# Fetching a channel's shifted columns one channel ahead, in three tiles, in the last stage of a four-layer convolution kernel

## The chip, the cores and the metric

The kernel runs on one core of one Trainium2 chip. The metric is the device time of one execution in microseconds (us). A core has five engines that run side by side, each with its own instruction queue: PE (matrix multiplication; PEld is its loading of weights), DVE (vector work), ACT (scalar functions and scaled copies), POOL (further vector work) and SP, which issues the transfers (DMA). An engine takes its queue in order: an instruction that waits holds everything behind it.

## What is computed

The input `x` has 32 images of 192 channels of 56 x 56 points, float32. Four layers follow, each of the form x + layer(group norm of x):

```python
x = x + _L0_conv_ref(_gn(x), ...)   # agent attention with a depthwise convolution
x = x + _L1_conv_ref(_gn(x), ...)   # scan in both directions (RWKV)
x = x + _L2_conv_ref(_gn(x), L2_conv_offset)
x = x + _L3_conv_ref(_gn(x), ...)   # long convolution, by Fourier transforms
```

Only layers 2 and 3 matter here; the last stage of the kernel computes both. Layer 2 shifts each group of four channels by whole rows and columns (zeros come in from outside) and smooths the result with a 3 x 3 Gaussian:

```python
out = jax.vmap(shift_one, in_axes=(1, 0, 0, 0), out_axes=1)(x, yc, xc, mask)
kern = jnp.exp(-sq / (2.0 * SIGMA ** 2))
kern = kern / kern.sum(axis=(1, 2), keepdims=True)
out_LO = jax.lax.conv_general_dilated(out, kern, ..., feature_group_count=Cn)
```

Layer 3 multiplies the two-dimensional spectrum of each channel by that of a 55 x 55 filter, transforms back, cuts out 56 x 56 and adds a bias times the input. The group norm before it takes mean and variance over six channels, so six channels make one group, and there are 32 groups.

## The kernel before

`all_blocks` (L1797) runs the filter, the attention and the scan first, which are not touched, and then `channel_blocks` (L1507), which begins at about 8360 us. Its 192 channels are worked on one by one. A tile holds one channel of all images: 114 partitions (two half-sets of images, each with 56 rows and one row of zeros) and 16 x 56 numbers in each.

For each channel the stage does this:

- `prepare(c)` (L1590). SP brings the channel into a tile `shifted` with its columns already displaced, by reading the source from another address (L1610). Where the displacement has brought in numbers of the neighbouring row, a second transfer writes zeros over them (L1613). It overwrites part of what the first wrote, so it waits until the first has landed. POOL multiplies the tile by the scale of the norm (L1614). ACT makes the first of three taps along the columns into a tile `smooth` (L1617). For the two other taps ACT makes a tile `more` (L1623) and POOL adds it to `smooth` (L1624); for channels 0, 2 and 4, DVE does both at once (L1620). `matrix` (L1552), once for four channels, builds the matrix that displaces the rows and taps along them.
- `shift` (L1628). SP loads the channel itself into a tile `x` (L1633), PE multiplies `smooth` by that matrix (L1639), DVE adds the product to `x` (L1640) and sums (L1641).
- `centre` (L1657). When all six channels of a group are shifted, DVE subtracts the mean into a tile `padded` (L1659), ACT squares it into `sq` (L1661) and DVE sums the squares (L1662).
- `analyse` (L1670) of the group before. PE transforms `padded` (L1785 in `_rows_to_spectra`, emptied from PSUM by ACT, L1791, and L1681), and DVE multiplies by the filter's spectrum in six instructions (L1688 to L1694).
- `synthesise` (L1697). PE transforms back (L1707, emptied from PSUM by ACT, L1715, and L1726), DVE adds to `x` (L1727), and SP stores the result by two transfers (L1730).

The loop at L1746 runs over groups and, inside, over six steps j. In step j it analyses channel j of the group before, synthesises the channel before that, shifts channels 2j and 2j + 1 of its own group while j < 3 (the shift half), centres two channels when j is 3 or more (the centre half), and prepares the channel four ahead of the step's number. Channels 0 to 3 are prepared ahead of the loop (L1744).

This order in the source is not the order of execution. A scheduler puts the instructions of every engine into a fixed order when the kernel is built: it takes what its own estimates of durations say is ready, earlier lines first. It also puts in the waits. Buffers matter to it: a tile that is made anew waits until the last use of the tile whose place it takes. There are two `shifted` tiles, taken in turn by channel number; five `smooth` tiles; three of the tag `spare`, which `more` and `sq` share; eight `padded` tiles, taken in turn; fifteen `x` tiles; and four PSUM tiles `ps`, which L1639, L1707, L1726, L1650, L1565 and L1785 share.

Of the kernel before, what the change touches and what calls it, by code (L numbers as in the profile page):

```python
# [20 lines left out]
F32 = mybir.dt.float32  # L21
# [7 lines left out]
C = 192  # L29
T = 96  # L30
S = 56
# [14 lines left out]
GROUP = C // 32  # L46
# [120 lines left out]
def _bc(ap, shape):  # L167

    return ap.unsqueeze(len(ap.shape)).to_broadcast(shape)
# [1337 lines left out]
def channel_blocks(ctx: ExitStack, tc: tile.TileContext, shifts, k, flat_x2, x2, rs2, spectra, out):  # L1507
# [10 lines left out]
    NI, NG = NB // 2, NB // 4  # L1518
    cp = ctx.enter_context(tc.tile_pool(name="d_c", bufs=1))
    xp = ctx.enter_context(tc.tile_pool(name="d_x", bufs=15))  # L1520
    wp = ctx.enter_context(tc.tile_pool(name="d_w", bufs=2))
# [3 lines left out]
    PR, NP = 2 * (S + 1), C // 4  # L1525
# [7 lines left out]
    for rows, shape in CHANNEL:  # L1533
        n = int(np.prod(shape))
        t = fixed[:rows, at : at + n]
# [2 lines left out]
    f1, f2, f3, f4, ones, ones_u, lags, diff_y, _ = pieces  # L1538
    eps = cp.tile([PR, 1], F32, name="eps", tag="eps")
    nc.vector.memset(eps, GN_EPS)  # L1540
    padded = [cp.tile([PR, NI, 64], F32, name=f"padded{i}", tag=f"padded{i}") for i in range(8)]
    for t in padded:
        nc.gpsimd.memset(t[:, :, S:64], 0.0)

    shifted = [cp.tile([PR, 2 * S * (NI + 2)], F32, name=f"shifted{i}", tag=f"shifted{i}") for i in range(2)]
    zeros = cp.tile([PR, S], F32, name="zeros", tag="zeros")
    for t in (*shifted, zeros):
        nc.gpsimd.memset(t, 0.0)
# [3 lines left out]
    def matrix(n):  # L1552

        if n not in made:
            engine = nc.vector if n < 2 else nc.gpsimd
            t = [wp.tile([PR, PR], F32, name=f"tap{f}", tag=f"tap{f}", bufs=1) for f in range(3)]
            for f in range(3):
                engine.tensor_scalar(
                    t[f], diff_y, found[:, n, 6 + f : 7 + f], found[:, n, 3 + f : 4 + f], ALU.is_equal, ALU.mult
                )  # L1560
            mat = wp.tile([PR, PR], F32, name="mat", tag="mat", bufs=3)
            engine.tensor_tensor(t[0], t[0], t[1], ALU.add)
            engine.tensor_tensor(mat, t[0], t[2], ALU.add)
            ps = psum()
            nc.tensor.matmul(ps[:PR, :PR], lags, mat, start=True, stop=True)  # L1565
            rows = wp.tile([PR, PR], F32, name="rows", tag="rows", bufs=3)
            nc.vector.tensor_copy(rows, ps[:PR, :PR])
            made.clear()
            made[n] = rows
        return made[n]  # L1570
# [7 lines left out]
    def begin(n):  # L1578
        q = Group()
        q.n, q.x, q.padded = n, [], []  # L1580
        q.scale = scales[n]
        q.g = sp.tile([84, GROUP, 2, 42], F32, name="g", tag="g")
        nc.sync.dma_start(out=q.g, in_=spectra[:, n * GROUP : (n + 1) * GROUP])
        q.sums = sp.tile([PR, 2, GROUP, NI], F32, name="sums", tag="sums")
        return q

    begin_at, scales, smooth, rows_of = {}, {}, {}, {}
    SPAN = PR * NI * S

    def prepare(c):  # L1590

        if c >= C:
            return
        n, j = divmod(c, GROUP)
        if j == 0:
            scales[n] = sp.tile([PR, GROUP, NI], F32, name="scale", tag="scale", bufs=3)
            for s in range(2):
                nc.sync.dma_start(
                    out=scales[n][(S + 1) * s : (S + 1) * (s + 1)],
                    in_=rs2[c : c + GROUP, s].partition_broadcast(S + 1),  # L1600
                )
        i = c // 4
        if c % 4 == 0:
            begin_at[i] = nc.values_load(
                begins[0:1, i : i + 1], engines=(mybir.EngineType.SP,), min_val=LEAD - S, max_val=LEAD + S
            )
        wide = shifted[c % len(shifted)]
        t = wide[:, 2 * S - 1 : 2 * S - 1 + 2 * S * NI].rearrange("p (g w) -> p g w", w=2 * S)[:, :, 0 : S + 2]
        there = flat_x2[bass.ds(begin_at[i] + c * SPAN, SPAN)].rearrange("(p g w) -> p g w", p=PR, w=S)
        nc.sync.dma_start(out=t[:, :, 1 : S + 1], in_=there)  # L1610

        bare = wide[:, bass.ds(LEAD + S - begin_at[i], 2 * S * (NI + 1))].rearrange("p (g w) -> p g w", w=2 * S)
        nc.sync.dma_start(out=bare[:, :, 0:S], in_=zeros.unsqueeze(1).to_broadcast([PR, NI + 1, S]))  # L1613
        nc.gpsimd.tensor_tensor(t, t, _bc(scales[n][:, j], [PR, NI, S + 2]), ALU.mult)  # L1614
        y = wp.tile([PR, NI, S], F32, name="smooth", tag="smooth", bufs=5)
        taps = [found[:, i, f : f + 1] for f in range(3)]
        nc.scalar.activation(y, t[:, :, 0:S], AF.Copy, scale=taps[0])  # L1617
        for f in (1, 2):
            if c < GROUP and c % 2 == 0:
                nc.vector.scalar_tensor_tensor(y, t[:, :, f : f + S], taps[f], y, ALU.mult, ALU.add)  # L1620
                continue
            more = wp.tile([PR, NI, S], F32, name="more", tag="spare", bufs=3)
            nc.scalar.activation(more, t[:, :, f : f + S], AF.Copy, scale=taps[f])  # L1623
            nc.gpsimd.tensor_tensor(y, y, more, ALU.add)  # L1624
        smooth[c] = y
        rows_of[c] = matrix(i)

    def shift(q, j):  # L1628

        c = q.n * GROUP + j  # L1630
        rows = rows_of.pop(c)
        x = xp.tile([PR, NI, S], F32, name="x", tag="x")
        nc.sync.dma_start(out=x, in_=x2[c].rearrange("s h g w -> (s h) g w"))  # L1633
        flat, y = x.rearrange("p g w -> p (g w)"), smooth.pop(c).rearrange("p g w -> p (g w)")
        for g0 in range(0, NI, 8):
            n = min(8, NI - g0)
            px = slice(g0 * S, (g0 + n) * S)
            ps = psum()
            nc.tensor.matmul(ps[:PR, : n * S], rows, y[:, px], start=True, stop=True)  # L1639
            nc.vector.tensor_tensor(flat[:, px], flat[:, px], ps[:PR, : n * S], ALU.add)  # L1640
        nc.vector.tensor_reduce(q.sums[:, 0, j, :], x, AX.X, ALU.add)  # L1641
        q.x.append(x)
        yield
# [21 lines left out]
    def spread(q):  # L1665
        q.rs = sp.tile([84, NI], F32, name="rs", tag="rs")
        nc.scalar.activation(q.rs, means(q, 1, ones_u), AF.Ln, bias=eps[:84])
        nc.scalar.activation(q.rs, q.rs, AF.Exp, scale=-0.5)
# [65 lines left out]
    def centres(q, j):  # L1734

        if j == 0:
            middle(q)
        centre(q, j)
        yield

    before, ending = None, iter(())
    for c in range(4):  # L1744
        prepare(c)
    for n in range(C // GROUP + 1):  # L1746
        q = begin(n) if n < C // GROUP else None
        for j in range(GROUP):
            two = [iter(()), iter(())]
            if q is not None:  # L1750
                two = [shift(q, 2 * j + i) if j < 3 else centres(q, 2 * j - 6 + i) for i in range(2)]
            taking = analyse(before, j) if before is not None else iter(())
            for step in (
                taking, two[0], taking, ending, ending, two[0], taking, ending, ending, two[1], taking,
                ending, two[1], ending,
            ):
                next(step, None)
            prepare(n * GROUP + j + 4)
            for rest in (*two, taking, ending):
                for _ in rest:  # L1760
                    pass
            ending = synthesise(before, j, before.product) if before is not None else iter(())
        if q is not None:
            spread(q)
        before = q
# [161 lines left out]
```

## Time and profile before

| what | us |
|---|---|
| median of three runs | 12290.15 |
| lowest and highest | 12282.31, 12302.48 |
| the profiled execution's own time | 12293.47 |
| its span, first to last instruction | 12291.7 |
| the channel stage in it, 8360 to the end | 3931.7 |
| PE, DVE, ACT, POOL busy in that stage | 3612.9, 3304.2, 2305.2, 1393.9 |
| from one group of six channels to the next, in the steady part | 119.3 |

The span is the sum of all stages, so the share of busy time over the whole of it says little of this one; the rows for the channel stage do. Idle time of an engine is named with what ended it, its releaser. A wait of an engine costs nothing unless another engine then stands still for it. SP's transfers are shown by the time of their issue and the time of landing.

### The profile page before, as it was taken

Reading aid. Unit: us, or ns where it says so; the run is one execution under the profiler, and the core shown is the slowest. Engines: PE = TensorE matmul, PEld = TensorE weight load, DVE = VectorE, ACT = ScalarE, POOL = GpSimd, SP = SyncE. Lnnn points to the kernel's source line nnn. Section 1 sums busy time; section 2 is a strip of 40 time slices with the busy share of each in tenths; the row PEclk is TensorE's granted clock in tenths of the full one; section 3 lists DMA queues with packets and bytes.
Section 4 is the critical chain, followed back from the end, with each engine's and each line's share of the span. In section 5 each row is a group of like instructions: output and inputs, shape, how many; then the busy total and the mean of one; then the engine's idle time right before and its main releaser. Section 6 shows DMA issues by size and latency. Waiting matters only on the chain. (4 is left out here: it accounts for less than half of the span.)

```text
span 12291.7 us, 158148 instructions
## 1 busy us (share of the span) xinstructions
PE 11099.2 (90%) x57358; PEld 6662.0 (54%) x57358; DVE 10776.0 (88%) x14739; ACT 7125.1 (58%) x14684; POOL 3379.2 (27%) x2551
## 2 busy tenths in 40 slices
PE   7999999999999999888888888886999999999999
PEld 3555555655555555333333333333666666666666
DVE  6888888888888887999999999995888888888887
ACT  3555555555555554566666666664565656656565
POOL 0000000000000000655655555553333433333330
PEclk9999999999999999899999999997999999999999
DMA  2111111111111111244344433444333333333331
GB/s 70 40 42 45 51 41 40 40 40 40 40 40 40 42 48 46 75 103 99 95 98 103 101 95 96 103 101 105 86 85 84 88 84 89 83 87 87 83 89 41
DMA packets 1652785, 881.51 MB, mean 72 GB/s; under 512 B 1492833, under 2 KB 1529972, under 8 KB 1642860
## 3 DMA queue, kind: packets, MB, share of 16 engines
q1 hardware_dynamic: 1641756, 845.59, 27.3%
q10 hardware_dynamic: 10240, 25.70, 0.8%
q8 instruction: 458, 7.50, 0.3%
q14 instruction: 331, 2.71, 0.1%
HBM read 482.13 MB, written 240.85 MB: 59 GB/s over the span
## 5 line engine op out<-in xcount | busy, mean ns | idle before, releaser
L617 DVE SCALAR_TENSOR_TENSOR o<-v_a,att_w,o 128x896 f32<-128x896 f32 (+1 forms) x1024 | 1056.6, 1032 | 418.5 <-ACT v_a L591 291.5
L1131 POOL MEMSET f<- 128x1 f32 x96 | 8.8, 98 | 4726.4 <-DMA st_c<-st 4721.4
L1791 ACT COPY y<-ps 64x252 f32<-64x252 f32 (+1 forms) x2376 | 805.3, 339 | 569.7 <-PE ps L1785 539.7
L1624 POOL TENSOR_TENSOR smooth<-smooth,more 114x896 f32<-114x896 f32 x378 | 864.3, 2289 | 909.7 <-ACT more L1623 832.9
L1707 PE MATMUL ps<-fixed,real 84*84 84x112 f32 x6144 | 1097.1, 260 | 0.9 <-ACT y L1791 0.9
L1707 PE MATMUL ps<-fixed,imag 84*84 84x112 f32 x6144 | 1094.1, 260 | 0.0
L1715 ACT ACTIVATE z<-ps,rs 84x112 f32<-84x112 f32 x3072 | 808.3, 356 | 250.2 <-PE ps L1707 247.2
L1707 PEld LDWEIGHTS ps<-fixed,real 84*84 84x84 f32 x6144 | 793.8, 154 | 163.6 <-issue 131.8
L1124 ACT ACTIVATE q<-q 128x784 f32<-128x784 f32 x384 | 328.3, 855 | 807.6 <-DVE q L1119 638.2
L1707 PEld LDWEIGHTS ps<-fixed,imag 84*84 84x84 f32 x6144 | 769.0, 154 | 0.0
L879 PE MATMUL ps<-sq,fixed 128*128 128x392 f32 x512 | 302.0, 753 | 427.3 <-ACT sq L1202 427.3
L634 ACT ACTIVATE pr<-ps,low 98x896 f32<-98x896 f32 (+1 forms) x384 | 352.0, 917 | 560.8 <-DVE low L632 560.1
L1614 POOL TENSOR_TENSOR shifted<-shifted,scale 114x928 f32<-114x928 f32 x192 | 362.8, 1889 | 1106.4 <-DMA shifted<-zeros 1070.0
L1785 PE MATMUL ps<-fixed,padded 114*128 114x168 f32 x3072 | 533.0, 325 | 138.9 <-DVE x L1727 135.5
L617 DVE SCALAR_TENSOR_TENSOR o<-v_c,att_w,o 128x448 f32<-128x448 f32 (+1 forms) x1024 | 638.1, 623 | 5.0
L630 PE MATMUL ps<-xs_a,gk_a 128*98 128x448 f32 (+1 forms) x1536 | 637.0, 495 | 0.0
L1726 PE MATMUL ps<-z,fixed 84*114 84x448 f32 x1536 | 619.2, 544 | 15.4 <-ACT z L1715 14.8
L631 PE MATMUL ps<-xs_c,gk_c 125*98 125x448 f32 (+1 forms) x1536 | 631.6, 492 | 0.0
L722 PE MATMUL ps<-gq_a,xs_a 128*112 128x294 f32 x1792 | 603.4, 418 | 19.3 <-DVE pq L727 19.3
L879 PE MATMUL ps<-x,weights 128*128 128x392 f32 x1536 | 573.2, 516 | 28.6 <-DVE bv L1153 14.3
L723 PE MATMUL ps<-gq_c,xs_c 125*112 125x294 f32 x1792 | 595.1, 413 | 0.0
L1785 PEld LDWEIGHTS ps<-fixed,padded 114*128 114x128 f32 x3072 | 481.3, 200 | 208.7 <-DVE x L1727 158.5
(377 smaller groups left out, 29242.6 us busy)
## 6 DMA issues: line engine op xcount, KB each, us to landing
x<-x SPq DMA_DIRECT2D x576, 392.0 KB
x<-x SPq DMA_DIRECT2D x512, 196.0 KB
shifted<-zeros SPq DMA_DIRECT2D x192, 423.9 KB
shifted<-x SPq DMA_DIRECT2D x192, 399.0 KB
x<-x SPq DMA_DIRECT2D x192, 399.0 KB
out_x<-x SPq DMA_DIRECT2D x384, 196.0 KB
x<-in_x SPq DMA_DIRECT2D x32, 1568.0 KB
x<-x SPq DMA_DIRECT2D x32, 1568.0 KB
```

The source lines that it names most:

```text
L617: nc.vector.scalar_tensor_tensor(dst, tap(i), dww[:, t, i : i + 1], dst, ALU.mult, ALU.add)
L630: mm(ps[P2, h, :n], g[:, cols], xs_a[j][:, px], start=True, stop=False)
L631: mm(ps[P2, h, :n], gk_c[0:KC, 2 * j + h, cols], xs_c[j][0:KC, px], start=False, stop=True)
L722: mm(ps[:SUB, i, :HA], xs_a[j][:, px], g, start=True, stop=False)
L723: mm(ps[:SUB, i, :HA], xs_c[j][0:KC, px], gq_c[0:KC, 2 * j + (q + i) // ns], start=False, stop=True)
L879: mm(out, aa, srcs[t][h], start=True, stop=False)
L1624: nc.gpsimd.tensor_tensor(y, y, more, ALU.add)
L1707: nc.tensor.matmul(ps[:84, i * 2 * S : (i + 1) * 2 * S], part[:, i0 + i].rearrange("p s u -> p (s u)"), f3[:, m, :], start=(m == 0), stop= ...
L1715: nc.scalar.activation(z[:, i0 + i].rearrange("p m w -> p (m w)"), ps[:84, i * 2 * S : (i + 1) * 2 * S], AF.Copy, scale=q.rs[:, i0 + i : i ...
L1726: nc.tensor.matmul(got, f4[:, m, :], z[:, i0 : i0 + n, m, :], start=(m == 0), stop=(m == 1))
L1785: nc.tensor.matmul(ps[:, g * 168 : (g + 1) * 168], flat[:, (g0 + g) * 128 : (g0 + g + 1) * 128], f1, start=True, stop=True)
L1791: nc.scalar.copy(y[64 * m : 64 * m + 64, 2 * g0 + i : 2 * (g0 + n) : 2], got[64 * i : 64 * i + 64, :, :, m, :])
```

## The change

`prepare` is cut in two. `fetch(c)` has the scale's loads, the address, the columns and the zeros. `prepare(c)` has the multiplication, the taps and the matrix. `fetch(0)` stands ahead of the loop; after that each `prepare(c)` has a `fetch(c + 1)` before it. The tiles `shifted` become three; the tiles `padded` become seven and `smooth` four. In each partition a `shifted` tile has 8064 bytes, a `padded` one 4096 and a `smooth` one 3584.

```diff
-    padded = [cp.tile([PR, NI, 64], F32, name=f"padded{i}", tag=f"padded{i}") for i in range(8)]
+    padded = [cp.tile([PR, NI, 64], F32, name=f"padded{i}", tag=f"padded{i}") for i in range(7)]
...
-    shifted = [cp.tile([PR, 2 * S * (NI + 2)], F32, name=f"shifted{i}", tag=f"shifted{i}") for i in range(2)]
+    shifted = [cp.tile([PR, 2 * S * (NI + 2)], F32, name=f"shifted{i}", tag=f"shifted{i}") for i in range(3)]
...
-    def prepare(c):
+    fetched = {}
+
+    def fetch(c):
 
         if c >= C:
             return
...
         nc.sync.dma_start(out=bare[:, :, 0:S], in_=zeros.unsqueeze(1).to_broadcast([PR, NI + 1, S]))
+        fetched[c] = t
+
+    def prepare(c):
+
+        if c >= C:
+            return
+        n, j = divmod(c, GROUP)
+        i, t = c // 4, fetched.pop(c)
         nc.gpsimd.tensor_tensor(t, t, _bc(scales[n][:, j], [PR, NI, S + 2]), ALU.mult)
-        y = wp.tile([PR, NI, S], F32, name="smooth", tag="smooth", bufs=5)
+        y = wp.tile([PR, NI, S], F32, name="smooth", tag="smooth", bufs=4)
...
     before, ending = None, iter(())
+    fetch(0)
     for c in range(4):
+        fetch(c + 1)
         prepare(c)
...
+            fetch(n * GROUP + j + 5)
             prepare(n * GROUP + j + 4)
```

## The prediction

> **What bounds the kernel now.** I read the page first, for the share of the stage and for the chain, then the busy times by stretch, then who waited for whom, and last the timeline of one group of six channels. From the page, engine totals and the lines of the chain:
>
> ```profile
> PE 11099.2 (90%) x57358; PEld 6662.0 (54%) x57358; DVE 10776.0 (88%) x14739; ACT 7125.1 (58%) x14684; POOL 3379.2 (27%) x2551
> PE ps L1707 4%; DMA shifted<-zeros 3%; DMA shifted<-x 3%; PE ps L1726 2%; PE re L1681 2%; PE ps L1785 2%; PE im L1681 2%; PE ps L1639 1%; DVE imag L1694 1%; DVE real L1690 1%; POOL shifted L1614 1%; POOL smooth L1624 1%; DVE padded L1659 1%; ACT y L1791 1%; DVE a L1693 1%
> ```
>
> 6% of 12291.7 us, some 740 us, of the chain are the two transfers that the change moves. That is not what they are worth: the chain follows the last arrival, and a path beside it can be nearly as late. So the busy times of the channel stage (us; PE, PEld, DVE, ACT, POOL busy; clock; DMA share, GB/s), first 28 groups of its steady part, then its start, then a stretch near the end where almost no preparing is left:
>
> ```profile
> 8716.00:12070.00 3354.00, 3154.74 (x18334) 2204.29 (x18333) 2909.68 (x4289) 2031.68 (x5464) 1231.32 (x699) 0.97 0.36 86
> 8373.00:8603.00 230.00, 139.56 (x616) 89.37 (x616) 136.44 (x193) 99.05 (x209) 111.40 (x74) 0.73 0.42 105
> 12075.00:12186.00 111.00, 110.12 (x680) 79.19 (x679) 95.34 (x155) 60.05 (x184) 6.16 (x3) 1.00 0.14 28
> ```
>
> PE is idle for 3354.0 - 3154.7 = 199 us of the steady part, 7.1 us in a group of 119.3 us (spacing of the loads of `g`). More than that no wait can give back. DVE is at 87%. The waits of the same 28 groups (engine, line, releaser: us, times, longest) name what makes up the 199 us, and what ACT stands still for:
>
> ```profile
> PE ps L1785 <- DVE x L1727: 126.4, 53, 4.5
> PE ps L1639 <- ACT z L1715: 29.4, 39, 2.1
> PE ps L1639 <- DVE x L1727: 15.9, 23, 1.2
> PE ps L1639 <- POOL smooth L1624: 9.2, 13, 0.8
> PE ps L1639 <- ACT y L1791: 6.5, 14, 2.2
> PE ps L1726 <- ACT z L1715: 5.8, 7, 2.2
> ACT smooth L1617 <- POOL shifted L1614: 439.5, 118, 7.3
> DVE sums L1662 <- ACT sq L1661: 48.0, 57, 1.2
> ```
>
> ACT stands 439.5 us (15.6 a group) in front of the first tap for a multiplication that is not done; behind it in its queue stand the copies that empty PSUM. PE, though, loses only 29.4 + 6.5 + 5.8 = 42 us to ACT (1.5 a group), and 142 us to DVE. One channel on the chain (start, us, what):
>
> ```profile
> 9287.66 6.29 DMA shifted<-x
> 9293.96 6.60 DMA shifted<-zeros
> 9300.70 1.77 POOL shifted L1614
> ```
>
> and POOL and ACT in the timeline at such a place (start, us, instruction, idle before it and releaser):
>
> ```profile
> 9580.22 2.21 POOL L1614 TENSOR_TENSOR shifted<-shifted,scale 114x928 f32<-114x928 f32 x1 [8.52 <-DMA shifted<-zeros]
> 9582.46 1.06 ACT L1617 ACTIVATE smooth<-shifted,found 114x896 f32<-114x896 f32 x1 [5.23 <-POOL shifted L1614]
> ```
>
> Zeros follow columns and the multiplication the zeros, 14.7 us in all; ACT, idle for 5.23 us, starts as POOL ends. The zeros cannot overlap the columns of the same tile, since they overwrite part of them.
>
> **The skill.** "DMA: Bandwidth & Descriptors", "Why a DMA increments its semaphore by 16 and not by 1": a transfer uses the largest number of engines up to 16 that divides its outer dimension; for 114 rows I work out 6. No view here shows engines one by one; 399 KB in 6.3 us agrees with a slow transfer. "SBUF — State Buffer", "Who interferes with whom": a DVE instruction with two SBUF inputs contends with a GpSimd one that reads SBUF. The trace agrees: L1694 takes 578 ns at least, 2496 at most, and about 2 us where POOL adds run beside it. "Perfetto Trace Analysis", "Identifying the Most-Contended Engine", warns that matmul busy share is no measure of roofline; I use gaps, not the share.
>
> **Step 1, columns and zeros start earlier.** Columns of channel c now wait for the tile of c-3 instead of c-2 (its last `more`, L1623). In the trace the columns of 63, 64, 65, 66 start at 9528.6, 9543.4, 9564.6, 9567.4, each within 0.1 us of the end of the last `more` of c-2. But tiles plus `smooth` tiles are seven before (2 + 5) and after (3 + 4). Where taps wait for `smooth`, the transfer's start is not earlier; the taps are one shift later (bursts of six shift matmuls, L1639, 10.5 us apart). Either way some 10 us lie between data and need, against 14.7 us plus SP's queue. I count the ACT stall as gone to seven tenths, not whole: POOL's order is fixed beforehand, and a multiplication placed too early still holds the adds behind it (L1624), which free `spare`. Worth: 0.7 x 1.5 = 1.1 us of PE a group. Of the 1.7 us a group for which DVE waits for `sq` (48.0/28) I take 0.3 as PE time, for DVE has no other idle there. Bounds: 0, and 1.5 + 1.7.
>
> **Step 2, `smooth` 5 to 4.** The first tap of c waits for the shift matmul of c-4, not c-5. For the fifth channel of a group the tap moves from 9558.7 to after its group's first shift (9574 to 9577). It is needed at 9615, its adds take 2 x 2.3 us after 3 x 1.05 us of ACT: over 25 us in hand, nothing late. Added wait: ACT for PE; behind it stand PSUM copies of matmuls that come after that shift anyway, so I take 0. Bounds: -0.3 (nothing in its place) to +0.5 us of PE for each of six passes, the second if PE is short of PSUM just then (four `ps`, and L1639 <- ACT already waits 2.1 us at the longest).
>
> **Step 3, POOL's adds of that channel move.** 4.6 us of L1624 leave the last tenth of the group, where DVE has no idle and PE 0.4 us, for the first shift, where DVE waits 1.6 us per 10 us. The durations of DVE's instructions above the tenth percentile of their own line and shape add up to 12.9 us a group; that is a third of a us per us of POOL in the centre half, a quarter in the shift half: -1.5 us of DVE there, +1.15 here. In PE time I take -0.3 and +0.3: 0.
>
> **Step 4, `padded` 8 to 7.** Centring channel c now waits for the analysis of c-7, an iteration (20 us) earlier: 0. If that were late, DVE would hold the centre half: up to +1 us a group.
>
> **Step 5, SP's queue.** The same 192 column and 192 zero transfers (0.85 us of issue each), moved one channel up, past x loads (L1633), scales and one pair of stores (L1730). The zeros' wait for landing (6.3 us) holds SP as before. The store may come some us later; x tiles are 15 deep and loads run up to 138 us ahead of their shift (9436.0 for 9574.2), so 0. Cover gone, each late load would cost its wait of 2.5 us (344.9/138).
>
> **Step 6, start and end.** From 8373 to 8603 the chain is columns, zeros, multiplication over and over, a new channel every 11 to 12 us. Three tiles let a third transfer queue up, but two issued back to back land about 4.2 us apart (the multiplications of channels 0 and 1, each waiting for its zeros, start at 8388.6 and 8392.8): 8.4 us a channel, and a load of x, for which I take 2.5 between 0 and 4.2. That is near 11 us, so the queue of transfers is nearly full. Group 0 gains 0; group 1 gains 1 us x 6 = 6. The third memset is 1.78 us on POOL, idle 2.6 us before its first multiplication: 0. After the last channel nothing changes.
>
> **Sum.** Steady: 1.1 + 0.3 = 1.4 us x 31 groups = 43, start 6: 49 us. Own time of the profiled execution 12293.5 (span 12291.7, 1.8 us around it) - 49 = 12244; that execution lies 3.3 us over the median of 12290.15, so 12241 for the median.
>
> **Rivals.** *Hidden anyway:* PE's largest wait, 126.4 us, is for DVE in the centre half, which no transfer touches; PE then waits a little longer there and the gain is under 24 us: 12280 (a fifth of 49 kept). For it: 142 of 199 us are DVE's. Against: the 42 us are PE's own idle, and nothing else fills them.
> *Other side, taps in step with PE:* each first tap now stands in ACT's queue behind a shift matmul, while that matmul needs a PSUM tile that ACT must empty. At 0.5 us for each of six passes, 3.0 us a group, less the 1.4 gained: 1.6 x 31 = 50 less 6 at the start, 44 slower: 12334. It decides from 1.4/6 = 0.23 us a pass. For it: L1639 is already where ACT's lateness hits PE. Against: what stands behind the tap mostly needs later matmuls.
> *More gained:* all 42 us of ACT, half of the `sq` wait, and the start by 20 us as group 1 closes up (its 8473 to 8603 is 130 us against 119): 42 x 31/28 + 27 + 20 = 93, 12197. For it: near the end, with no preparing, PE is at 110.1 of 111 us. Against: there POOL is quiet too.
> *Not what it says:* the order on the engines is fixed beforehand by estimated durations, and the transfers could be put no earlier; that is the first rival's time.
>
> **Chances.** Forecast 0.46 (own range 12200 to 12265), hidden 0.22, slower 0.23, more gained 0.09. A measurement of this kernel tells about 0.2%, 25 us, from no change. Faster 0.46 + 0.09 = 0.55; same 0.22; slower 0.23. The range runs from 12185, within the last case, to 12325, into the slower case, leaving about 0.17 out.
>
> **What would show it.** Right: ACT's wait at the first tap for the multiplication falls from 15.6 us a group below 5, PE's waits for ACT below 0.6, group spacing near 117.9 us. Step 2 wrong: ACT's first tap waits for L1639, and PE's L1639 for ACT above 1.5 us a group. Step 3 wrong: L1694 grows. Step 5 wrong: x loads land after their shift is due. Wrong as a whole: spacing unchanged although the ACT wait is gone.

## The result, and the profile after

| | before | after |
|---|---|---|
| median, us (5 runs each) | 12289.5 | 12355.6 |
| lowest and highest | 12282.3, 12302.5 | 12338.3, 12358.8 |
| ratio, 95% interval | | 1.0051 [1.0036, 1.0065] |
| span of the profiled execution | 12291.7 | 12336.5 |
| from one load of `g` to the next, mean of 29 groups | 119.47 | 121.19 |

The change made the kernel slower by about 0.5%, 63 us by the ratio or 66 by the medians. First the engine totals and the lines of the chain from the page of the changed kernel. Line numbers have moved: the first tap is now L1626, the passes into `more` L1632, the adds L1633, the multiplication L1623, the shift's matmul L1648, PSUM's copies L1803 and L1724.

```profile
PE 11099.2 (90%) x57358; PEld 6656.5 (54%) x57358; DVE 10766.9 (87%) x14739; ACT 7141.9 (58%) x14684; POOL 3323.3 (27%) x2551
...
PE ps L1716 6%; PE ps L1735 2%; PE re L1690 2%; PE im L1690 2%; DMA shifted<-zeros 2%; DMA shifted<-x 2%; ACT y L1803 2%; PE ps L1797 2%; PE ps L1648 2%; DVE padded L1668 1%; DVE imag L1703 1%; POOL smooth L1633 1%; DVE real L1699 1%; DVE sums L1671 1%; DVE a L1702 1%; DVE a L1701 1%
```

The two transfers have gone from 6% of the chain to 4%, as the change meant, and the time went up all the same. PE's busy time over the whole program is the same to 0.1 us, but that hides a difference. In the channel stage the same 20832 matmuls are busy for 3627.7 us instead of 3612.9: 15 of the 50 us by which the stage grew, counted from its load of `found`. The other 35 us are idle time of PE, in which the waits show; the last section comes back to the 15. The channel stage, and then the same steady stretch as before the change, in the columns of the prediction:

```profile
8360.00:12336.50 3976.50, 3627.68 (x20832) 2531.85 (x20832) 3295.19 (x4897) 2321.96 (x6202) 1393.80 (x811) 0.95 0.35 83
...
8716.00:12070.00 3354.00, 3121.58 (x18007) 2178.78 (x18007) 2850.30 (x4213) 2008.09 (x5362) 1205.83 (x687) 0.96 0.36 84
```

In the steady stretch PE is busy 33 us less in the same time. The waits in it (engine, line, releaser: us, times, longest), ACT's first, then PE's:

```profile
ACT more L1632 <- POOL smooth L1633: 313.7, 87, 9.9
...
ACT smooth L1626 <- PE ps L1648: 17.3, 36, 0.7
...
PE ps L1797 <- DVE x L1736: 106.5, 44, 5.0
PE ps L1648 <- ACT y L1803: 38.1, 14, 4.3
PE ps L1648 <- POOL mat L1563: 35.5, 11, 4.8
PE ps L1648 <- ACT z L1724: 25.5, 28, 2.4
PE ps L1648 <- DVE x L1736: 13.6, 31, 1.1
PE ps L1648 <- POOL smooth L1633: 8.2, 3, 7.0
```

The wait of 439.5 us at the first tap for the multiplication is off the list. In its place stands one that the kernel before did not have: ACT waits 313.7 us at `more` for POOL's adds. And PE, which lost 61 us in front of the shift's matmul, now loses 121 there; its idle time in the stretch went from 199 to 232 us, from 7.1 to 8.4 us a group.

The timeline of ACT over the first shifts of a group shows how (start, us, instruction, idle before it and releaser):

```profile
9554.99 2.00 ACT L1632 ACTIVATE more<-shifted,found 114x896 f32<-114x896 f32 x2
...
9557.81 1.07 ACT L1632 ACTIVATE more<-shifted,found 114x896 f32<-114x896 f32 x1
...
9568.90 1.06 ACT L1626 ACTIVATE smooth<-shifted,found 114x896 f32<-114x896 f32 x1
9573.29 1.06 ACT L1632 ACTIVATE more<-shifted,found 114x896 f32<-114x896 f32 x1 [3.33 <-POOL smooth L1633]
...
9589.29 1.05 ACT L1632 ACTIVATE more<-shifted,found 114x896 f32<-114x896 f32 x1 [7.51 <-POOL smooth L1633]
9590.25 4.21 ACT L1803 COPY y<-ps 64x252 f32<-64x252 f32 x12
```

POOL in the same stretch:

```profile
9569.03 1.76 POOL L1623 TENSOR_TENSOR shifted<-shifted,scale 114x928 f32<-114x928 f32 x1 [12.65 <-DMA shifted<-zeros]
9570.75 4.92 POOL L1633 TENSOR_TENSOR smooth<-smooth,more 114x896 f32<-114x896 f32 x2
9585.02 1.76 POOL L1623 TENSOR_TENSOR shifted<-shifted,scale 114x928 f32<-114x928 f32 x1 [9.36 <-DMA shifted<-zeros]
9586.74 4.67 POOL L1633 TENSOR_TENSOR smooth<-smooth,more 114x896 f32<-114x896 f32 x2
```

Read it from the top. At 9554.99 ACT makes both `more` tiles of channel 64, but its first tap has no `smooth` tile yet: that tile is held until the group's first shift, and the tap runs at 9568.90. Nothing can be added to a tap that is not there, so the two `more` tiles are held for about 14 us before the first add can start. At 9557.81 channel 65 takes the third and last tile of the tag `spare`. Its second pass has to wait for an add of channel 64. The adds of 65 in turn stand in POOL's queue behind a multiplication, two channels later, that waits 9.36 us for its transfer. So ACT stands 7.51 us, and behind it the copies that empty PSUM. Four of them end at about 9591.7, and PE starts its third shift:

```profile
9591.82 2.74 PE L1648 MATMUL ps<-smooth,rows 114*114 114x448 f32 x4 [3.08 <-POOL mat L1563]
```

Its releaser is given as a POOL instruction that ends at 9591.80, but that is a coincidence. In the trace the entry of PE's queue just ahead of this matmul waits for a counter (a semaphore) of ACT from 9587.91 to 9591.77, and it is ACT's fourth copy, ending at 9591.72, that raises this counter; POOL's is asked for only after it. It is the same for all 11 waits put down to L1563 and the three put down to L1633, and for the 13 put down to L1624 in the kernel before. So of the 121 us in front of the shift's matmul 107 are waits for copies by ACT (38.1 + 35.5 + 25.5 + 8.2), where it was 45 of 61. None of them is left in e6 below, where POOL still makes the same matrices.

### The profile page after: what moved, and what is told of

Same layout as the page of the kernel before. It is cut to its first block, busy times and chain, and to the rows that moved or that the text cites. A ratio compares the mean times of both kernels' runs of the same rounds, so it can differ in the third digit from the quotient of the medians.

```text
span 12336.5 us, 158145 instructions
## 1 busy us (share of the span) xinstructions
PE 11099.2 (90%) x57358; PEld 6656.5 (54%) x57358; DVE 10766.9 (87%) x14739; ACT 7141.9 (58%) x14684; POOL 3323.3 (27%) x2551
## 3 DMA queue, kind: packets, MB, share of 16 engines
q14 instruction: 331, 2.71, 0.1%
## 5 line engine op out<-in xcount | busy, mean ns | idle before, releaser
L1803 ACT COPY y<-ps 64x252 f32<-64x252 f32 (+1 forms) x2376 | 805.3, 339 | 604.2 <-PE ps L1797 574.5
L1633 POOL TENSOR_TENSOR smooth<-smooth,more 114x896 f32<-114x896 f32 x378 | 879.0, 2325 | 769.6 <-ACT more L1632 650.0
L1724 ACT ACTIVATE z<-ps,rs 84x112 f32<-84x112 f32 x3072 | 811.4, 356 | 353.8 <-PE ps L1716 352.0
L1623 POOL TENSOR_TENSOR shifted<-shifted,scale 114x928 f32<-114x928 f32 x192 | 355.0, 1849 | 1344.9 <-DMA shifted<-zeros 1320.6
L1649 DVE TENSOR_TENSOR x<-x,ps 114x448 f32<-114x448 f32 x384 | 236.7, 619 | 401.9 <-PE ps L1648 366.9
```

The costliest lines, as they stand in the source:

```text
L1724: nc.scalar.activation(z[:, i0 + i].rearrange("p m w -> p (m w)"), ps[:84, i * 2 * S : (i + 1) * 2 * S], AF.Copy, scale=q.rs[:, i0 + i : i ...
L1803: nc.scalar.copy(y[64 * m : 64 * m + 64, 2 * g0 + i : 2 * (g0 + n) : 2], got[64 * i : 64 * i + 64, :, :, m, :])
```

## The experiments

Theory A put the loss on the fourth `smooth` tile, theory B on the third `shifted` tile with the earlier transfers. All ratios are to the kernel before, run on the same chip beside it.

| run | what it is | ratio, 95% interval | median, us | before there |
|---|---|---|---|---|
| changed kernel | the change as it stands above | 1.0051 [1.0036, 1.0065] | 12355.6 | 12289.5 |
| e1 | before, with 4 `smooth` | 1.0073 [1.0059, 1.0086] | 12385.9 | 12294.4 |
| e2 | changed, with 5 `smooth` and 14 `x` | 0.9991 [0.9985, 0.9998] | 12283.0 | 12294.4 |
| e3 | tiles as before, transfers ahead in the source | 0.9998 [0.9989, 1.0006] | 12292.5 | 12294.4 |
| e4 | tiles as changed, transfers not ahead in the source | 1.0032 [1.0019, 1.0046] | 12339.5 | 12294.4 |
| e5 | changed, adds ahead of a later multiplication on POOL | 0.9952 [0.9939, 0.9966] | 12241.1 | 12302.8 |
| e6 | changed, passes into `more` behind the first tap on ACT | 0.9904 [0.9889, 0.9919] | 12181.1 | 12302.8 |
| e7 | changed, with 4 `spare` and 14 `x` | 0.9920 [0.9905, 0.9936] | 12200.6 | 12302.8 |
| e8 | e2 with e6's order | 0.9929 [0.9915, 0.9942] | 12215.5 | 12302.8 |
| e9 | before, with e6's order | 0.9998 [0.9989, 1.0007] | 12294.8 | 12295.2 |
| e10 | e1 with e6's order | 0.9917 [0.9900, 0.9933] | 12191.0 | 12295.2 |
| e11 | changed, with the orders of e5 and e6 | 0.9933 [0.9916, 0.9949] | 12213.2 | 12295.2 |
| e12 | before, with 14 `x` | 0.9996 [0.9987, 1.0004] | 12287.1 | 12295.2 |

### The parts of the change one by one: e1 to e4

e1 is the kernel before with one number changed:

```diff
-        y = wp.tile([PR, NI, S], F32, name="smooth", tag="smooth", bufs=5)
+        y = wp.tile([PR, NI, S], F32, name="smooth", tag="smooth", bufs=4)
```

> The kernel before with four smooth tiles instead of five, nothing else: two shifted tiles, eight padded tiles, no separate fetch. Theory A (the fourth smooth tile makes the loss: taps wait for the shift of four channels earlier, the multiplications stand ahead of the adds on POOL, and ACT waits for the adds): slower than before by 40 to 90 us, and ACT's wait for L1624 at L1623 appears, 200 us or more in the 28 steady groups, against 0 before. Theory B (three tiles and the earlier transfers make the loss, by putting multiplications that wait for a transfer earlier into POOL's queue): within 20 us of before.

It alone is slower by 0.73%, at least as much as the whole change (the two intervals overlap a little). The waits of e1, ACT's and then PE's:

```profile
ACT more L1623 <- POOL shifted L1614: 247.2, 56, 8.8
...
ACT more L1623 <- POOL smooth L1624: 65.0, 30, 2.6
...
PE ps L1639 <- ACT y L1791: 72.4, 14, 5.5
PE ps L1639 <- POOL tap L1558: 70.7, 13, 6.4
```

The size is at the upper end of what theory A said. The wait for the adds is only 65.0 us, not 200; most of ACT's time at `more` is spent on the multiplication, since with two `shifted` tiles it too comes late. Both stand at the passes into `more`, with the copies for PSUM behind them in ACT's queue; of PE's 70.7 us put down to L1558, 66.6 are again waits for ACT's copies. So held `spare` tiles are not the larger wait of e1. What it shares with the changed kernel is the order on ACT: for 89 of the 192 channels, in both traces, ACT makes two or three passes into `more` before the first tap of that channel (its own two, and sometimes one of the next). In the kernel before it makes one, for 30 channels. PE and DVE have the same order in e1 as before. That ACT's order carries the loss of e1 is what e10 below shows; by which of its waits was not taken apart.

e2 is the changed kernel with the fifth tile back, and the room for it taken from the `x` tiles:

```diff
-    xp = ctx.enter_context(tc.tile_pool(name="d_x", bufs=15))
+    xp = ctx.enter_context(tc.tile_pool(name="d_x", bufs=14))
...
-        y = wp.tile([PR, NI, S], F32, name="smooth", tag="smooth", bufs=4)
+        y = wp.tile([PR, NI, S], F32, name="smooth", tag="smooth", bufs=5)
```

> The changed kernel with five smooth tiles again, room for it taken from the x tiles (14 instead of 15). Theory A: the loss is gone, 12230 to 12295 us, and what the earlier transfers are worth alone shows: ACT's wait for the multiplication at the first tap under 150 us in 28 groups. Theory B: slower than before by 40 us or more, as in the changed kernel.

The loss is gone, and what is left of the change is worth 0.09%. Its waits show why no more:

```profile
ACT more L1632 <- POOL shifted L1623: 117.7, 28, 5.7
...
PE ps L1648 <- ACT z L1724: 71.8, 28, 4.6
```

The wait at the first tap has moved to a `more` pass, once a group, and once a group PE loses 2.6 us. Here too passes stand ahead of their tap, for 59 channels.

e3 has the transfers ahead in the source, but two `shifted`, eight `padded` and five `smooth` tiles; e4 has the tiles of the changed kernel, and the transfers back in `prepare`.

```diff
# e3, against the changed kernel
-    padded = [cp.tile([PR, NI, 64], F32, name=f"padded{i}", tag=f"padded{i}") for i in range(7)]
+    padded = [cp.tile([PR, NI, 64], F32, name=f"padded{i}", tag=f"padded{i}") for i in range(8)]
...
-    shifted = [cp.tile([PR, 2 * S * (NI + 2)], F32, name=f"shifted{i}", tag=f"shifted{i}") for i in range(3)]
+    shifted = [cp.tile([PR, 2 * S * (NI + 2)], F32, name=f"shifted{i}", tag=f"shifted{i}") for i in range(2)]
...
-        y = wp.tile([PR, NI, S], F32, name="smooth", tag="smooth", bufs=4)
+        y = wp.tile([PR, NI, S], F32, name="smooth", tag="smooth", bufs=5)
# e4, against the kernel before
-    padded = [cp.tile([PR, NI, 64], F32, name=f"padded{i}", tag=f"padded{i}") for i in range(8)]
+    padded = [cp.tile([PR, NI, 64], F32, name=f"padded{i}", tag=f"padded{i}") for i in range(7)]
...
-    shifted = [cp.tile([PR, 2 * S * (NI + 2)], F32, name=f"shifted{i}", tag=f"shifted{i}") for i in range(2)]
+    shifted = [cp.tile([PR, 2 * S * (NI + 2)], F32, name=f"shifted{i}", tag=f"shifted{i}") for i in range(3)]
...
-        y = wp.tile([PR, NI, S], F32, name="smooth", tag="smooth", bufs=5)
+        y = wp.tile([PR, NI, S], F32, name="smooth", tag="smooth", bufs=4)
```

> The transfers stand a channel ahead in the source, but with two shifted tiles, eight padded and five smooth tiles as before. Theory A: within 20 us of before, since the tile decides when the transfer can start, not the place in the source. Theory B, if the place in the source counts: slower by 20 us or more.

> Three shifted tiles, seven padded and four smooth tiles as in the changed kernel, but the transfers stay with the multiplication in the source. Theory A: like the changed kernel, 12335 to 12370 us, since tiles and smooth are the same. Theory B, if the place in the source counts: at least 30 us faster than the changed kernel.

Where the transfers stand in the source does nothing (e3), and without it the changed kernel's tiles are nearly as slow (e4; its interval and the changed kernel's overlap). The tile decides when a transfer can start. So the change is, for the chip, a third `shifted` tile paid for with a `smooth` tile, and the payment costs more than the tile brings: +0.73% in e1, of which e4, with the third tile, keeps +0.32%. The number of `padded` tiles was not varied alone; e2 has seven and no loss.

### How the fourth tile costs time: e5, e6, e7

Three edits to the changed kernel, each on another link of the loop seen in the timeline. In the traces PE and DVE have the order of the changed kernel in all three, and in e7 POOL too. e5 puts the multiplication of channel c behind the second add of channel c-2 in POOL's queue:

```diff
-        nc.gpsimd.tensor_tensor(t, t, _bc(scales[n][:, j], [PR, NI, S + 2]), ALU.mult)
+        if c - 2 in added:
+            with tc.issue_after(added.pop(c - 2).ins):
+                nc.gpsimd.tensor_tensor(t, t, _bc(scales[n][:, j], [PR, NI, S + 2]), ALU.mult)
...
-            nc.gpsimd.tensor_tensor(y, y, more, ALU.add)
+            added[c] = nc.gpsimd.tensor_tensor(y, y, more, ALU.add)
```

> The changed kernel, with each multiplication (L1623) put into POOL's queue behind the second add (L1633) of the channel two before it; PE and DVE keep their orders. Theory A1 (with four smooth tiles the loss is that adds stand on POOL behind a multiplication that waits for its transfer): at least half of the 61 us is healed, 12325 us or less, and ACT's wait for L1633 falls from 313.7 us in 28 groups below 120. Theory A2 (the loss is that two more tiles are made ahead of the first tap and hold the spare tiles): less than 20 us healed.

e6 puts the passes into `more` behind the first tap of the same channel in ACT's queue:

```diff
-        nc.scalar.activation(y, t[:, :, 0:S], AF.Copy, scale=taps[0])
+        first = nc.scalar.activation(y, t[:, :, 0:S], AF.Copy, scale=taps[0])
...
-            nc.scalar.activation(more, t[:, :, f : f + S], AF.Copy, scale=taps[f])
+            with tc.issue_after(first.ins):
+                nc.scalar.activation(more, t[:, :, f : f + S], AF.Copy, scale=taps[f])
```

> The changed kernel, with the two more passes (L1632) put into ACT's queue behind the first tap (L1626) of the same channel; PE and DVE keep their orders. Theory A2: at least half of the 61 us is healed, 12325 us or less, and ACT's wait for L1633 falls below 120 us in 28 groups. Theory A1: less than 20 us healed.

e7 has a fourth `spare` tile and 14 `x` tiles:

```diff
-            more = wp.tile([PR, NI, S], F32, name="more", tag="spare", bufs=3)
+            more = wp.tile([PR, NI, S], F32, name="more", tag="spare", bufs=4)
...
-        sq = wp.tile([PR, NI, S], F32, name="sq", tag="spare", bufs=3)
+        sq = wp.tile([PR, NI, S], F32, name="sq", tag="spare", bufs=4)
```

> The changed kernel with four spare tiles instead of three, room from the x tiles (14 instead of 15); POOL, PE and DVE keep their orders. Both A1 and A2 pass through the spare tiles, so both expect ACT's wait for L1633 to fall below 200 us in 28 groups and 15 to 45 us healed. If that wait is not what PE loses by (theory A3: the late tap itself, or the matrix for the shift standing on POOL), the wait falls and the time stays within 10 us of the changed kernel.

All three heal more than the whole loss: from +0.51% to -0.48%, -0.96% and -0.80%. The two readings between which e5 and e6 were to decide, the adds behind a waiting multiplication (A1) and the `more` tiles made ahead of the tap (A2), are not rivals, then, but links of one loop, and any of them opens it. e7 was expected to gain 15 to 45 us and gained about 160. ACT's wait for the adds, 313.7 us in the changed kernel, is 124.9 in e5 and 123.0 in e7 (a near miss of the bound of 120 in e5), and in e6 it is 1.0, once. ACT in e6, over the shifts of a group:

```profile
9541.87 1.06 ACT L1626 ACTIVATE smooth<-shifted,found 114x896 f32<-114x896 f32 x1 [0.43 <-PE ps L1649]
9542.84 1.98 ACT L1633 ACTIVATE more<-shifted,found 114x896 f32<-114x896 f32 x2
9547.64 4.22 ACT L1804 COPY y<-ps 64x252 f32<-64x252 f32 x12 [2.83 <-PE ps L1798]
9551.89 1.06 ACT L1626 ACTIVATE smooth<-shifted,found 114x896 f32<-114x896 f32 x1
```

and what is left of its waits, ACT's first tap and then PE:

```profile
ACT smooth L1626 <- PE ps L1649: 24.8, 57, 0.4
...
PE ps L1798 <- DVE x L1737: 134.7, 53, 5.1
PE ps L1649 <- DVE x L1737: 10.6, 26, 0.9
PE re L1691 <- ACT y L1804: 3.5, 23, 0.2
```

The tap waits at most 0.4 us for its shift, its passes come after it, and PE loses 3.5 us to ACT in the whole stretch, where it lost 44 in the kernel before (the 42 of the prediction, and 2.6 in front of L1681; 53 with the 9.2 put down to L1624). POOL still waits 1181.9 us for transfers in e6, against 1196.4 in the changed kernel: no cost of that wait is to be seen once ACT hardly waits for an add behind it.

### What the order and the tiles are worth apart: e8 to e12

The edits are those shown already, in other company: e8 is e2 with e6's edit of the order; e9 is the kernel before with it; e10 is e1 with it; e11 is the changed kernel with the edits of e5 and e6; e12 is the kernel before with 14 `x` tiles, the control for e2, e7 and e8.

> The changed kernel with five smooth tiles, 14 x tiles, and the two more passes behind the first tap in ACT's queue; only ACT's order differs from e2. In e2 ACT waits 117.7 us in 28 groups at L1632 for the multiplication, and PE's L1648 waits 71.8 us for ACT's L1724. If the first is what makes the second, this version is 15 to 60 us faster than e2 and beats both kernels, 12225 to 12270 us; if not, it is within 10 us of e2.

> The kernel before with the two more passes behind the first tap in ACT's queue; only ACT's order changes, and five smooth tiles leave the first tap little to wait for. If the ordering alone makes the 122 us gain of e6 over the kernel before: 12230 us or less. If it needs the changed kernel's tiles: within 30 us of the kernel before, and ACT's wait for the multiplication at the first tap stays above 300 us in 28 groups.

> The kernel of e1 (before, with four smooth tiles) with the two more passes behind the first tap. If the loss of e1 (91 us) is the holding of spare tiles: at least half of it is healed, 12345 us or less where the kernel before stands at 12295. What lies between this kernel and e6 is then the worth of the third shifted tile with its earlier transfers; for that I expect 20 to 80 us.

> The changed kernel with both orders, adds ahead of later multiplications on POOL (e5) and more passes behind the first tap on ACT (e6). ACT waits for no add in e6 any more, so if that wait is the whole way by which POOL's order cost time: within 15 us of e6, or up to 25 us slower because the multiplications then start later.

> The kernel before with 14 x tiles instead of 15 and nothing else (the control for e2, e7 and e8): loads of x run over 100 us ahead, so within 15 us of the kernel before.

e12 is neutral. e8 beats both kernels, and e2 by 76 us by the ratios, where at most 60 were expected; of the four engines' orders only ACT's differs between these two. e9 shows that the order alone does nothing for the kernel before. Few passes stood ahead of their tap there, and this line of ACT's waits says what is left: with five tiles the tap is held by the multiplication, which the order does not touch.

```profile
ACT smooth L1617 <- POOL shifted L1614: 447.3, 144, 7.3
```

With four tiles (e10) the same order turns e1's +0.73% into -0.83%, still with two `shifted` tiles. The same line of its waits:

```profile
ACT smooth L1617 <- POOL shifted L1614: 171.6, 77, 6.3
```

e6 has the third tile besides, and none of that wait; the two ratios, 0.9917 and 0.9904, have intervals that overlap. The third tile with its transfers is worth 10 us by the medians there and 16 by the ratios, less than the 20 to 80 expected, and cannot be told from nothing. With five `smooth` tiles it is another matter: e8 against e9, 0.9929 against 0.9998, makes it worth 0.7%, some 85 us, once the passes stand behind their tap (e8 also has seven `padded` and 14 `x` tiles). Either the third `shifted` tile or the step from five `smooth` tiles to four takes much of the tap's wait for the multiplication away (447.3 us in e9; 4.9 in e8, 171.6 in e10), and the second of them finds less left.

e11 is slower than e6 by 0.3%, with intervals that just touch, and misses its bound by some 10 us: with multiplications held back, ACT waits for them again (121.5 us at the first tap), so e5's order seems to cost something once it has nothing to heal.

The fastest version is e6, the changed kernel with its passes behind the first tap: 0.96% faster than the kernel before.

## Why the prediction was wrong, point by point

- *The step that failed is step 2.* It took the fourth `smooth` tile at 0, with "nothing late" and over 25 us in hand. The wait it looked at, of the tap for the shift, is as harmless as it took it to be: 17.3 us in 28 groups, 0.7 at the longest. It looked at one instruction too few. Of ACT's three only the first tap needs a `smooth` tile; the two passes beside it need `spare` tiles, which were free, so the scheduler put them first, where they held those tiles and stood waiting in front of the copies for PSUM. The price with the kernel before as its base (e1): 122.58 - 119.47 = 3.1 us a group; with the other tiles of the changed kernel (e2 as the base) 121.19 - 118.87 = 2.3. Of the two signs named for this step one came: PE's wait for ACT at the shift's matmul is 2.3 us a group by the releasers named, and 3.9 with those put down to POOL, against a bound of 1.5. The other, ACT's wait at the tap, stayed at 0.6.
- *Step 1* was right in direction: the wait of 15.6 us a group at the first tap is gone. Its discount named POOL's order, adds held behind a multiplication and `spare` tiles not freed, but as a remainder of three tenths of a wait. It was the way by which the loss came. With five `smooth` tiles the whole change brings only 0.09%, some 11 us (e2), where the sum has 49. But the transfers were not overrated: the passes ahead of their taps hid what they bring, as e8 shows with some 85 us.
- *Step 3:* DVE's time above the tenth percentile of each line and shape comes to 12.7 us a group in both traces. L1694 means 932 ns before and, as L1703, 948 after. 0 was right.
- *Step 4:* no wait of DVE for an analysis is among those found. *Step 5:* neither PE nor DVE waits for a load of x in the steady stretch, and the place of the transfers in SP's order brought nothing (e3).
- *Step 6:* from the load of `found` to the third load of `g`, 237.4 us became 235.6: 1.8 us gained, not 6. The end, from the last load of `g`, took 223.7 us instead of 221.6; this was not foreseen.
- *The sum* in the profiled execution: 29 x 1.72 = 50 us in the steady part, -1.8 at the start, +2.1 at the end. The stages ahead, which nothing touches, took 5.3 us less there. Together 45 us, the difference of the two spans.
- *The rival on the other side* came out near in time, 12334 us, by another mechanism. It had ACT wait at the tap for the shift's matmul while the matmul wanted PSUM. Its end is what happened, PE without PSUM that ACT had still to empty; but ACT stood at the passes, for POOL's adds, and not at the tap. That the time is near is luck.

## What to carry to other kernels

When a buffer is made scarcer, follow every instruction of the same item of work, not only the one that allocates it: a scheduler that takes what is ready will put those that can run without it early, and they hold whatever they need until the late one comes. A wait that keeps step with the bound engine is cheap (0.4 us at the longest in e6), while one on a queue of another pace, here transfers through POOL, was not (9.9 us at the longest in the changed kernel). And a tile taken away can be a gain, if the order of what depends on it is stated.

## What the runs showed that was not expected

Four `smooth` tiles are better than five once the order is stated, in two pairs: e10 against e9 (0.9917 against 0.9998) and e6 against e8 (0.9904 against 0.9929, with 15 `x` tiles against 14; these two intervals just touch). For the first pair the waits suggest a reason: the tap then waits for the shift instead of standing ahead of copies while a multiplication is late (447.3 us in e9, 171.6 in e10). No run took it apart further. For the second pair that cannot be it, since in e8 the tap waits only 4.9 us for the multiplication; its cause stays open.

In e6 PE's idle time is 152 us of the 3354, at 115.88 us a group: 5.3 us a group against 7.1 before. The rest of the 3.6 us a group lies in busy time, 110.6 us against 112.4, for the same matmuls. The granted clock in the stretch is 0.98 against 0.97, and 0.96 in the changed kernel.

The traces tie this clock to PE's waits. Two shifts of the changed kernel, the second behind a wait, and three slices of 2 us around the second (the clock is the third number from the right):

```profile
9565.87 1.67 PE L1648 MATMUL ps<-smooth,rows 114*114 114x448 f32 x4
...
9577.97 2.71 PE L1648 MATMUL ps<-smooth,rows 114*114 114x448 f32 x4 [1.48 <-ACT z L1724]
```

```profile
9574.00:9576.00 2.00, 2.00 (x24) 2.00 (x22) 2.00 (x5) 0.65 (x2) 1.67 (x1) 1.00 0.48 111
...
9578.00:9580.00 2.00, 2.00 (x4) 0.94 (x5) 0.62 (x1) 2.00 (x10) 0.00 (x0) 0.69 0.42 114
9580.00:9582.00 2.00, 2.00 (x3) 0.53 (x2) 1.25 (x2) 1.78 (x4) 0.00 (x0) 0.50 0.49 112
```

Behind the wait the clock is at half, and the four matmuls of the shift take 2.71 us instead of 1.67. In the steady stretch the clock is either whole or at half, nearly always for 3.4 or 6.8 us at a time: 36 times in the kernel before, 52 in the changed kernel, 56 in e1 and 29 in e6. Over the steady stretch of the 14 traces, 363 of the 382 waits of PE above 3 us have such a drop begin between their start and 1.5 us after their end, and 22 of the 1047 below 1 us. Between 1 and 3 us it is now one, now the other (6 of 24 in the kernel before, 23 of 33 in the changed kernel). So a long wait of PE costs more than its own length, and part of the gains and losses here is the clock's; how much was not measured by itself.
